# A selective scan's third output block, summed and copied out by other engines

## The chip, the cores and the metric

The kernel runs on one core of a Trainium2 chip. The metric is the device time of one execution in microseconds (us), the median of several runs. The core has five engines that run their own instruction queues in order[...]: TensorE (PE in the profile, its weight loads PEld), VectorE (DVE), ScalarE (ACT), GpSimd (POOL), and SyncE (SP), which here only issues DMA transfers.

## The reference

The input is eight images of 384 channels and 64 x 64 pixels, in fp32. Two layers follow each other, each of the form x + f(groupnorm(x)). The first f is an attention over channels with 1x1 and depthwise 3x3 convolutions. The second is a selective scan in four directions; the change lies there. In its code, cut down:

```python
xs = _cross_scan(x)                       # rows, columns, and both reversed
x_dbl = einsum('bkdl,kcd->bkcl', xs, x_proj_weight)
dts, Bs, Cs = split(x_dbl)                # 12, 16 and 16 channels
dt = softplus(einsum(dts, dt_projs_weight) + dt_projs_bias)
def step(h, inp):                         # over the 4096 places
    dA = exp(dt * A)
    h = h * dA + (dt * u)[..., None] * B
    y = einsum('bkdn,bkn->bkd', h, C)
ys = scan(step) + Ds * u
y = _cross_merge(ys)                      # the four directions are added
```

A layernorm over channels and a GELU end the layer. What matters here is the last line: the outputs of four sweeps over the image are summed place by place.

## The kernel before, in words

`selective_scan` handles one image. The loop is over 32 **steps**: four sweeps (k = 0 to 3; sweeps 2 and 3 run backwards), each over eight chunks of 512 places. Steps 0 to 7 are sweep 0, 8 to 15 sweep 1, and so on. In even sweeps the view of x is contiguous; in odd ones (columns) it is strided. A step has 12 **units**: three blocks of 128 channels (j) times four groups of four states (g). Unit r of a step is j = r // 4, g = r % 4.

For a unit, POOL forms the products db = w * B for its four states (`drive`, L910). ScalarE forms the decays da by an exponential, one per state (`decay`, L898), into one of three PSUM banks. VectorE runs the four scans (L922), each 512 places long, into h. One unit later TensorE transposes h in four banks of 4 x 128 columns (`turn`, L943; two banks in rotation), ScalarE copies each bank to SBUF as hc (`keep`, L949), and TensorE multiplies hc with the laid-out C and accumulates over the four groups into a PSUM bank py, one bank for each block j (`add_up`, L960). A direct term with D joins it in even sweeps (L966).

py has two banks, so a block's bank has to be emptied before the next block but one begins. `take` empties it: in sweep 0 VectorE copies it to SBUF (L1000); in later sweeps it adds it to the partial sum of the earlier sweeps (L1002). That sum has been fetched from memory into a buffer ysum by `sum_of` (L988, three buffers); the result is stored again (L986), and both go through SP's queue. The first two blocks of a step are taken in its unit 9, the third in the **next** step's unit 4.

Other work hangs on certain units. In units 0 to 3 TensorE projects the next step's x, three matmuls in each unit (`project`, L810), and reads x in the next step's view, so strided where the next step is in an odd sweep. In unit 4 ScalarE copies that projection out (`lay_out`, L818), and DMA spreads it as B and C. In unit 9, the burst, TensorE forms the next step's dt (L864, three 128x512 matmuls), ScalarE applies the softplus with two table loads (L872), and VectorE forms four tiles of C (L849). In steps 29 to 31 of all but the last image VectorE also collects the next image's statistics.

The order on each engine is written out by hand: `pin` keeps instructions in program order. Within a unit ScalarE alternates exponentials for two scans ahead with copies hc; VectorE's third scan of a unit needs the exponential issued just before that unit's first copy, and the fourth the one just after it:

```python
                turned(0)
                scanned(0)
                added(3, o - 1)
                if r == 4 and s > 0 and not last:
                    take(s - 1, 2)
                decay(i0 + 2)
                kept(0)
                turned(1)
```

Here `o` is the unit before. In units 0 to 3 the projection stands after `kept(1)`, ahead of the third transposes. DMA issues are not pinned.

Of the kernel before, what the change touches and what calls it, by code (L numbers as in the profile page):

```python
# [17 lines left out]
NJ = C // P  # L18
# [14 lines left out]
NG = N // NV  # L33
# [3 lines left out]
NLB = CH // P  # L37
# [58 lines left out]
def tile_channel_attention_then_selective_scan(ctx: ExitStack, tc: tile.TileContext, a: dict):  # L96
    nc = tc.nc
# [7 lines left out]
    ident = const.tile([P, P], F32, name="ident")  # L105
# [12 lines left out]
    for name in ("dt_bias", "Ds", "ln_w", "ln_b", "temp"):  # L118
        t = const.tile(list(a[name].shape), F32, name=name)
# [624 lines left out]
    def selective_scan(b, x1, stats1):  # L744

        y_d = dram.tile([L, C], F32, tag="yd", bufs=2, name=f"yd{b}")
        with ExitStack() as st:
# [6 lines left out]
            pin = tc.keep_in_program_order  # L754
# [11 lines left out]
            with tc.tile_pool(name=f"sn{b}", bufs=1, reuse_waits="tile") as np_:  # L766
# [4 lines left out]
                for c in range(5):  # L771
                    for j in range(NJ):
                        s = x1[j][:, bass.ts(c, CH)]
# [19 lines left out]
            steps = []  # L793
# [3 lines left out]
            S = len(steps)  # L797
# [85 lines left out]
            das, dbs, hs, hcs, pts, pys, carries, sums = {}, {}, {}, {}, {}, {}, {}, {}  # L883

            def place(u):

                s, r = divmod(u, UN)
                return s, *divmod(r, NG)
# [24 lines left out]
            def scan(u, v):  # L913
                s, j, g = place(u)
                k, c, start, end = steps[s]
                n = NV * g + v
                if v == 0:
                    hs[u] = work.tile([P, CH, NV], F32, tag="h", bufs=3, name=f"h{b}_{u}")
                da, db, h = das.pop(NV * u + v), dbs[u][:, v, :], hs[u][:, :, v]
                if k >= 2:  # L920
                    da, db, h = da[:, ::-1], db[:, ::-1], h[:, ::-1]
                pin(nc.vector.tensor_tensor_scan(  # L922
                    h, da, db, 0.0 if start else carries[s - 1][:, j, n : n + 1],
                    ALU.mult, ALU.add,
                ))
# [12 lines left out]
            def turn(u, lb):  # L938

                t = ps_t.tile([P, NF, P], F32, tag="t", name=f"pt{b}_{u}_{lb}")  # L940
                for f in range(NF):
                    q = NF * lb + f
                    pin(nc.tensor.transpose(t[:, f, :], hs[u][:, bass.ts(q, HP), :].rearrange("p l v -> p (l v)"), ident))  # L943
                pts[u, lb] = t

            def keep(u, lb):

                t = work.tile([P, NF, P], F32, tag="hc", bufs=6, name=f"hc{b}_{u}_{lb}")
                pin(nc.scalar.copy(t, pts.pop((u, lb))))  # L949
                hcs[u, lb] = t  # L950

            def add_up(u, lb):

                s, j, g = place(u)
                if g == lb == 0:
                    pys[s, j] = ps_y.tile([P, NLB, P], F32, tag="py", name=f"py{b}_{s}_{j}")
                hc, py = hcs.pop((u, lb)), pys[s, j]
                for f in range(NF):
                    q = NF * lb + f
                    pin(nc.tensor.matmul(  # L960
                        py[f * HP : (f + 1) * HP, lb, :], lhsT=cps[s, g][:, q, :], rhs=hc[:, f, :],
                        start=g == lb == 0, stop=g == NG - 1 and lb == NLB - 1,
                    ))
                k, c = steps[s][:2]
                if g == 1 and lb in SKIPS.get(k, ()):
                    pin(nc.tensor.matmul(  # L966
                        py[:, lb, :], lhsT=x1[j][:, c * CH + lb * P : c * CH + (lb + 1) * P],
                        rhs=skip[:, j, :], start=False, stop=False,
                    ))

            def rows(k, c, j):

                cs = bass.ts(j, P)
                if k % 2 == 0:
                    yield slice(0, P), y_d[bass.ts(c, CH), cs].rearrange("(l p) c -> p l c", p=P)
                    return
                v = y_d.rearrange("(h w) c -> h w c", w=W)[:, bass.ts(c, CH // H), cs]
                v = v.rearrange("h (l f) c -> f h l c", f=2)
                for f in range(2):
                    yield slice(f * H, (f + 1) * H), v[f]  # L980

            def move_y(s, j, t, store):
                k, c = steps[s][:2]
                for part, r in rows(k, c, j):
                    if store:
                        nc.sync.dma_start(r, t[part])  # L986
                    else:
                        nc.sync.dma_start(t[part], r)  # L988

            def sum_of(s, j):  # L990

                sums[s, j] = work.tile([P, NLB, P], F32, tag="ysum", bufs=3, name=f"ys{b}_{s}_{j}")
                if steps[s][0] > 0:
                    move_y(s, j, sums[s, j], False)

            def take(s, j):

                t = sums.pop((s, j))
                if steps[s][0] == 0:
                    pin(nc.vector.tensor_copy(t, pys.pop((s, j))))  # L1000
                else:
                    pin(nc.vector.tensor_add(t, t, pys.pop((s, j))))  # L1002
                move_y(s, j, t, True)
# [17 lines left out]
            for c in range(5, NCH):  # L1021
                for j in range(NJ):
                    s = x1[j][:, bass.ts(c, CH)]
# [36 lines left out]
            def unit(u):  # L1060

                o = u - 1
                s, r = divmod(u, UN)
                nxt = s + 1 < S
                last = u == U
                burst = r == 9 and nxt
                i0 = NV * u

                def scanned(v):
                    if not last:  # L1070
                        scan(u, v)

                def turned(lb):
                    if o >= 0:
                        turn(o, lb)

                def kept(lb):
                    if o >= 0:
                        keep(o, lb)

                def added(lb, of=o):
                    if of >= 0:
                        add_up(of, lb)

                if r in (2, 6, 10) and not last:
                    sum_of(s, r // 4)
                if not nxt and r in (8, 10) and not last:
                    take(s, (r - 8) // 2)
                if r >= 8 and nxt:
                    fetch(s + 1, r - 8)  # L1090

                if not last:
                    drive(u + 1)
                if u >= 2:
                    keep_last(u - 2)
                if r == 7 and nxt:
                    mingle_c(s + 1)
                if r == 10 and nxt:
                    weigh(s + 1, 0)
                if 0 < s < S and r in (0, 2):  # L1100
                    weigh(s, 1 + r // 2)

                turned(0)
                scanned(0)
                added(3, o - 1)
                if r == 4 and s > 0 and not last:
                    take(s - 1, 2)
                decay(i0 + 2)
                kept(0)
                turned(1)  # L1110
                if r == 8 and nxt:
                    turn_c(s + 1)
                scanned(1)
                decay(i0 + 3)
                if burst:
                    take(s, 0)
                    pd0 = step_matmul(s + 1, 0)
                    kept(1)
                    pd1 = step_matmul(s + 1, 1)
                    pd2 = step_matmul(s + 1, 2)  # L1120
                    added(0)
                    for j, pd in enumerate((pd0, pd1, pd2)):
                        step_size(s + 1, j, pd)
                    scanned(2)
                    scanned(3)
                    decay(i0 + 4)
                    for g in range(NG):
                        spread_c(s + 1, g)
                    take(s, 1)
                    added(1)  # L1130
                    turned(2)
                    decay(i0 + 5)
                    kept(2)
                    turned(3)
                    kept(3)
                    added(2)
                    return
                kept(1)
                if nxt and r < 4:
                    for i in range(3):  # L1140
                        project(s + 1, 3 * r + i)
                turned(2)
                added(0)
                scanned(2)
                decay(i0 + 4)
                kept(2)
                turned(3)
                added(1)
                if r == 4 and nxt:
                    lay_out(s + 1)  # L1150
                scanned(3)
                decay(i0 + 5)
                kept(3)
                added(2)
# [77 lines left out]
    for b in range(B):  # L1232
        x1, x1_d, stats1 = channel_attention(b, *x, before)
        y_d, x = selective_scan(b, x1, stats1)
        before = (b, x1_d, y_d)
# [50 lines left out]
```

## Time and profile before

| | us |
|---|---|
| median of 3 runs (19570.98 to 19581.24) | 19573.84 |
| the profiled execution's own time | 19593.03 |
| its span in the profile | 19591.2 |
| VectorE busy | 18453.4 (94%) |
| ScalarE busy | 17584.1 (90%) |
| TensorE busy | 17097.0 (87%) |
| GpSimd busy | 16874.4 (86%) |

A group in the profile is written as line, engine, operation, output <- inputs, shape and count; then the busy time in us, the mean of one in ns, and the idle time of the engine just before such instructions with what ended it. In the timeline the columns are start and duration in us, then the instructions merged (x4), with the idle time ahead of them in brackets. An fp32 matmul appears as two records[...]. TensorE's durations overlap each other; the distance between starts is what one costs.

### The profile page before, as it was taken

The page shows a single profiled execution, that of the slowest core. Times are in us where ns is not written, and L with a number is a line of the kernel's source. Part 1 is how long each engine was busy: PE and PEld are TensorE (multiplying, and loading weights), DVE is VectorE, ACT ScalarE, POOL GpSimd, SP SyncE. Part 2 cuts the span into 40 slices and gives each one's busy share as a digit, 9 for nine tenths or more (in the row PEclk, how much of TensorE's full clock was granted, in tenths as well). Part 3 has the DMA queues.
Part 4 walks back from the last instruction along what each step waited for, and adds up shares of the span by engine and source line. Part 5 has one row for each costly group of instructions (what it writes and reads, how often), then busy time and mean ns, then how long its engine had stood idle before and what let it go on. Part 6 is the DMA issues. An engine that isn't in the chain of part 4 may idle for free.

```text
span 19591.2 us, 415258 instructions
## 1 busy us (share of the span) xinstructions
PE 17097.0 (87%) x166560; PEld 10219.2 (52%) x166560; DVE 18453.4 (94%) x17510; ACT 17584.1 (90%) x30011; POOL 16874.4 (86%) x7486
## 2 busy tenths in 40 slices
PE   7888888888888888888888888888888888888887
PEld 4555545555455554555545555455554555545554
DVE  7999989999899998999989999899998999989998
ACT  6999979999799987999879998899988999889998
POOL 4999959999599985999859998599985999869997
PEclk9999999999999999999999999999999999999998
DMA  1232322223222232232322323223232223322223
GB/s 47 84 97 97 112 89 83 94 97 111 91 86 94 95 109 89 87 97 96 109 85 87 97 97 108 85 87 97 97 108 92 83 95 97 106 93 88 94 93 124
DMA packets 1214410, 1849.25 MB, mean 94 GB/s; under 512 B 154209, under 2 KB 1018721, under 8 KB 1075265
## 3 DMA queue, kind: packets, MB, share of 16 engines
q1 hardware_dynamic: 1211616, 1822.57, 28.7%
q8 instruction: 1314, 21.53, 0.5%
q14 instruction: 616, 5.04, 0.1%
q10 hardware_dynamic: 864, 0.12, 0.0%
HBM read 1503.58 MB, written 318.77 MB: 93 GB/s over the span
## 4 chain that ended last, share of the span: by engine, by line
ACT 27%; PE 23%; DVE 15%; issue 4%; POOL 3%; DMA 1%; SPq 0%; DVEq 0%; ACTq 0%; POOLq 0%
ACT da L898 12%; ACT hc L949 10%; PE pt L943 10%; DVE h L922 10%; PE py L960 5%; PE px L810 3%; DVE ac L451 3%; POOL db L910 2%; ACT dt L872 1%; PE pp L599 1%; PE pd L864 1%; PE py L966 1%; ACT pr L413 1%; ACT L872 1%; ACT L898 1%
## 5 line engine op out<-in xcount | busy, mean ns | idle before, releaser
L910 POOL TENSOR_TENSOR db<-w,B 128x2048 f32<-128x2048 f32 x3072 | 14053.0, 4578 | 618.8 <-DVE h L922 514.7
L922 DVE TENSOR_TENSOR_SCAN h<-da,ca,db 128x512 f32<-128x512 f32 x10752 | 12786.6, 1263 | 305.3 <-ACT da L898 287.0
L898 ACT ACTIVATE da<-dt,neg_a 128x512 f32<-128x512 f32 x12288 | 8741.8, 713 | 157.6 <-DVE h L922 153.4
L943 PE MATMUL pt<-ident,h 128*128 128x128 f32 x49152 | 8127.0, 294 | 858.4 <-DVE h L922 505.8
L949 ACT COPY hc<-pt 128x512 f32<-128x512 f32 x12288 | 7393.0, 604 | 704.7 <-PE pt L943 641.1
L943 PEld LDWEIGHTS pt<-ident,h 128*128 128x128 f32 x49152 | 5452.3, 146 | 3314.2 <-issue 1912.0
L960 PE MATMUL py<-hc,cp 128*32 128x128 f32 x98304 | 5070.4, 290 | 893.4 <-ACT hc L949 726.0
L960 PEld LDWEIGHTS py<-hc,cp 128*32 128x32 f32 x98304 | 2050.1, 110 | 3164.5 <-ACT hc L949 1607.1
L922 DVE TENSOR_TENSOR_SCAN h<-da,db 128x512 f32<-128x512 f32 x1536 | 1748.2, 1206 | 115.8 <-ACT da L898 73.5
L420 POOL TENSOR_TENSOR pr<-pr,pr 128x1008 f32<-128x1008 f32 x288 | 673.3, 2338 | 1201.1 <-ACT pr L413 1184.0
L810 PE MATMUL px<-x,wx 128*44 128x128 f32 x6144 | 1219.8, 343 | 36.9 <-DVE cp L849 21.3
L881 POOL TENSOR_TENSOR w<-x,dt 128x512 f32<-128x512 f32 x744 | 1062.4, 1428 | 33.4 <-ACT dt L872 31.9
L810 PEld LDWEIGHTS px<-x,wx 128*44 128x44 f32 x6144 | 687.4, 128 | 367.0 <-issue 190.0
L864 PE MATMUL pd<-xd,wdt 128*128 128x512 f32 x1536 | 731.8, 613 | 157.0 <-DVE h L922 151.2
L426 POOL TENSOR_TENSOR pr<-pr,pr 128x1008 f32<-128x1008 f32 x288 | 574.8, 1996 | 277.2 <-ACT pr L413 193.8
L849 DVE TENSOR_TENSOR cp<-quad,pct 128x512 f32<-128x512 f32 x1024 | 628.2, 674 | 10.9 <-PE pct L838 10.9
L599 PE MATMUL pp<-v,mT 128*128 128x512 f32 x1152 | 539.1, 618 | 92.5 <-DVE v L456 91.4
L872 ACT ACT_TABLE_LOAD x256 | 328.4, 1283 | 229.1 <-PE pd L864 228.1
L936 POOL COPY ca<-h 128x4 f32<-128x4 f32 x2688 | 531.6, 198 | 0.0
L864 PEld LDWEIGHTS pd<-xd,wdt 128*128 128x128 f32 x1536 | 272.3, 190 | 465.4 <-issue 239.2
L872 ACT ACTIVATE dt<-pd,dt_bias 128x512 f32<-128x512 f32 x768 | 475.0, 686 | 8.2 <-PE pd L864 4.4
L1002 DVE TENSOR_TENSOR ys<-ys,py 128x512 f32<-128x512 f32 x576 | 383.9, 667 | 34.6 <-PE py L960 34.6
(334 smaller groups left out, 11500.5 us busy)
## 6 DMA issues: line engine op xcount, KB each, us to landing
B<-bcd SPq DMA_DIRECT2D x1024, 1024.0 KB, 4.8
yd<-ys SPq DMA_DIRECT2D x384, 256.0 KB, 3.4
ys<-yd SPq DMA_DIRECT2D x768, 128.0 KB, 2.9
yd<-ys SPq DMA_DIRECT2D x768, 128.0 KB, 4.3
x<-in_x SPq DMA_DIRECT2D x48, 1024.0 KB, 7.2
x1d<-x SPq DMA_DIRECT2D x192, 256.0 KB, 2.8
ys<-yd SPq DMA_DIRECT2D x192, 256.0 KB, 3.0
fy<-yd SPq DMA_DIRECT2D x128, 384.0 KB, 3.8
```

The lines of the kernel that those rows point to most:

```text
L420: pin(nc.gpsimd.tensor_add(q[:, :, 1:], q[:, :, 1:], left[:, :, : W - 1]))
L599: pin(nc.tensor.matmul(pps[m, c], lhsT=fold_of[0][:, j, bass.ts(m, P)], rhs=vs["v"][:, j, bass.ts(c, CH)], start=j == 0, stop=j == NJ - 1,))
L810: pin(nc.tensor.matmul(split(pxs[s][:XR, :])[:, part, :], lhsT=wx[:, j, k, :], rhs=view(x1[j], k, c)[:, part, :], start=i == 0, stop=i == ...
L864: pin(nc.tensor.matmul(pd, lhsT=wdt[:, k, bass.ts(j, P)], rhs=xds[s], start=True, stop=True))
L872: pin(nc.scalar.activation(dts[s, j], pd, AF.Softplus, bias=small["dt_bias"][:, j, k : k + 1]))
L881: pin(eng.tensor_mul(split(ws[s, j]), view(x1[j], k, c), split(dts[s, j])))
L898: pin(nc.scalar.activation(t, dts[s, j], AF.Exp, scale=neg_a[:, j, steps[s][0], n : n + 1]))
L910: pin(eng.tensor_mul(t, w.broadcast_to([P, NV, CH]), bts[s, g]))
L922: pin(nc.vector.tensor_tensor_scan(h, da, db, 0.0 if start else carries[s - 1][:, j, n : n + 1], ALU.mult, ALU.add,))
L943: pin(nc.tensor.transpose(t[:, f, :], hs[u][:, bass.ts(q, HP), :].rearrange("p l v -> p (l v)"), ident))
L949: pin(nc.scalar.copy(t, pts.pop((u, lb))))
L960: pin(nc.tensor.matmul(py[f * HP : (f + 1) * HP, lb, :], lhsT=cps[s, g][:, q, :], rhs=hc[:, f, :], start=g == lb == 0, stop=g == NG - 1 an ...
```

## The change

The third block of every step that is followed by another, so 31 of 32 in each image, is no longer taken by VectorE in unit 4. In sweeps 1 to 3 TensorE adds the fetched partial sum to the bank py in unit 1 of the next step, as a matmul with the identity, 128x512 fp32, that closes the accumulation. In unit 2 ScalarE copies the bank into the same ysum buffer, and the store follows. In sweep 0 there is nothing to add, and only the copy moves to ScalarE. The first two blocks of a step, and the last step's third, are taken as before.

```diff
                 hc, py = hcs.pop((u, lb)), pys[s, j]
+                full = g == NG - 1 and lb == NLB - 1 and not summed_by_pe(s, j)
...
-                        start=g == lb == 0, stop=g == NG - 1 and lb == NLB - 1,
+                        start=g == lb == 0, stop=full,
...
+            def summed_by_pe(s, j):
+                return j == NJ - 1 and s < S - 1 and steps[s][0] > 0
+
+            def sum_by_pe(s, j):
+
+                if summed_by_pe(s, j):
+                    pin(nc.tensor.matmul(
+                        pys[s, j].rearrange("p b c -> p (b c)"), lhsT=ident,
+                        rhs=sums[s, j].rearrange("p b c -> p (b c)"), start=False, stop=True,
+                    ))
+
+            def take_by_act(s, j):
+
+                t = sums.pop((s, j))
+                pin(nc.scalar.copy(t, pys.pop((s, j))))
+                move_y(s, j, t, True)
...
                 added(3, o - 1)
-                if r == 4 and s > 0 and not last:
-                    take(s - 1, 2)
+                if r == 1 and s > 0:
+                    sum_by_pe(s - 1, 2)
                 decay(i0 + 2)
                 kept(0)
+                if r == 2 and s > 0 and not last:
+                    take_by_act(s - 1, 2)
                 turned(1)
```

## The prediction

> **What bounds the kernel now.** I read the page's engine shares and groups first.
>
> ```profile
> PE 17097.0 (87%) x166560; PEld 10219.2 (52%) x166560; DVE 18453.4 (94%) x17510; ACT 17584.1 (90%) x30011; POOL 16874.4 (86%) x7486
> ...
> L922 DVE TENSOR_TENSOR_SCAN h<-da,ca,db 128x512 f32<-128x512 f32 x10752 | 12786.6, 1263 | 305.3 <-ACT da L898 287.0
> ...
> L949 ACT COPY hc<-pt 128x512 f32<-128x512 f32 x12288 | 7393.0, 604 | 704.7 <-PE pt L943 641.1
> ...
> L1002 DVE TENSOR_TENSOR ys<-ys,py 128x512 f32<-128x512 f32 x576 | 383.9, 667 | 34.6 <-PE py L960 34.6
> ```
>
> VectorE is fullest, and inside the scan it almost never rests: 12288 scans leave 421 us of gaps (305.3 + 115.8, the first steps' scans). Next the list of waits, to see what makes those gaps:
>
> ```profile
> ACT hc L949 <- PE pt L943: 641.1, 1283, 3.6
> ...
> DVE h L922 <- ACT da L898: 360.5, 791, 2.6
> ```
>
> VectorE waits for ScalarE's exponential, and ScalarE, in order, waits for TensorE's transposes. The timeline says where. TensorE in unit 2 of step 12 of the fourth image (next step in sweep 1, whose x view is strided):
>
> ```profile
> 8517.92 0.66 PE L943 MATMUL pt<-ident,h 128*128 128x128 f32 x4
> 8518.50 0.43 PE L960 MATMUL py<-hc,cp 128*32 128x128 f32 x8
> 8518.86 0.66 PE L943 MATMUL pt<-ident,h 128*128 128x128 f32 x4
> 8519.45 0.65 PE L960 MATMUL py<-hc,cp 128*32 128x128 f32 x16
> 8520.02 0.66 PE L943 MATMUL pt<-ident,h 128*128 128x128 f32 x4
> 8520.61 0.43 PE L960 MATMUL py<-hc,cp 128*32 128x128 f32 x8
> 8520.97 0.65 PE L943 MATMUL pt<-ident,h 128*128 128x128 f32 x4
> 8521.55 1.48 PE L810 MATMUL px<-x,wx 128*44 128x128 f32 x6
> 8522.96 0.66 PE L943 MATMUL pt<-ident,h 128*128 128x128 f32 x4
> ```
>
> No gap: the same transpose returns after 8522.96 - 8517.92 = 5.04 us, of which 1.41 are the projection (L810), while VectorE's four scans take 4 x 1.175 = 4.70. So in units 0 to 3 of such a step TensorE is the slowest; ScalarE waits for it once a unit:
>
> ```profile
> 8523.71 0.59 ACT L949 COPY hc<-pt 128x512 f32<-128x512 f32 x1 [0.55 <-PE pt L943]
> ```
>
> VectorE then reaches unit 4 with hardly any exponential in hand:
>
> ```profile
> 8529.69 0.66 DVE L1002 TENSOR_TENSOR ys<-ys,py 128x512 f32<-128x512 f32 x1
> 8530.27 5.98 DVE L922 TENSOR_TENSOR_SCAN h<-da,ca,db 128x512 f32<-128x512 f32 x5
> ```
>
> The fifth of these scans starts at 8534.99; its exponential ran 8534.09 to 8534.80: 0.19 in hand. Where the next step's view is contiguous, three projections take 0.78, a unit costs TensorE about 4.4, and VectorE runs unbroken to the add and past it (step 18):
>
> ```profile
> 8871.95 24.79 DVE L922 TENSOR_TENSOR_SCAN h<-da,ca,db 128x512 f32<-128x512 f32 x21 [0.40 <-ACT da L898]
> 8896.66 0.66 DVE L1002 TENSOR_TENSOR ys<-ys,py 128x512 f32<-128x512 f32 x1
> ```
>
> There exponentials lie ready about 1.0 us early in unit 2 and 1.1 in unit 5. From unit 6 on all steps are VectorE's; unit 9's burst sets ScalarE back to VectorE's pace. So a step's change is what VectorE has lost or won by unit 5.
>
> [...]
>
> **The change, part by part.** Per image, steps 1 to 31 have the third block's take moved: 31 x 8 = 248.
>
> Removed: one VectorE operation in unit 4. Its 0.66 overlaps the next scan; on the path it is 8530.27 - 8529.69 = 0.58 us. 248 x 0.58 = 144 us, if VectorE can use it.
>
> Added to TensorE, in steps 9 to 31 (184 times): a 128x512 fp32 matmul in unit 1, after the last py of the old block and ahead of the second transposes. The nearest row is L864 (same shape): [...]their weight loads 0.43 apart, so 0.86 us. Ends: 0.75 (some overlap) to 1.1 (a wait for the loaded y in front of it). I take 0.86. Behind it stand transposes, ScalarE's copies, then exponentials, then scans. The y that it reads was fetched some nine units earlier, in unit 4 of the step before, so its landing is no limit.
>
> Added to ScalarE: a copy PSUM to SBUF 128x512 in unit 2, between a copy hc and an exponential, 248 times. L949's next instruction starts 0.48 after it[...], and L949's mean is 604. I take 0.48 (0.45 to 0.6).
>
> Moved: the store of the block (one DMA issue, two in odd sweeps) on SP, from behind VectorE's add in unit 4 to behind ScalarE's copy in unit 2. Behind it in SP's queue stand the load into the same ysum buffer and the bcd store, whose data come from ScalarE in unit 4 as before; both can only go earlier. The py bank and the ysum buffer come free two units sooner. POOL's instructions and their order stay, and its products are finished 1.1 us or more, mostly 3 us, before their scan; a step shorter by 0.58 takes no more than that from the lead each time, and POOL idles about 2 us per step (514.7 us for VectorE over 256 steps) to make it up. I cost all these at nothing; with that cover gone, each us that POOL is late would be one of the step.
>
> Now VectorE's delay by unit 5, step by step (- is a gain). "In hand" is a scan's start less the end of its exponential, as the timeline before has them, in means over the eight images.
> - Steps 1 to 6: no matmul. ScalarE is 0.48 late, and 0.7 or more lies ready: hidden. -0.58 each, 6 steps, -3.5.
> - Steps 7 and 8: no matmul, strided. The 0.55 gap swallows the copy, but exponentials are only 0.03 early in unit 5 already, so the freed 0.58 is waited away. 0.
> - Steps 9 to 14 and 25 to 28: TensorE full, strided. In unit 2 ScalarE is 0.86 + 0.48 late; the 0.55 gap takes the copy's share back, 0.86 stays. VectorE is 0.86 late in unit 3, wins 0.58 back in unit 4, and loses it in unit 5: 0.14 in hand on average, of which 0.03 is the least ever seen, so 0.86 - 0.11 = +0.75. 10 steps, +7.5.
> - Steps 15 and 17 to 22: contiguous. ScalarE has no gap in unit 2: transposes come 0.86 later, 0.3 of it spare, plus 0.48: 1.1 late against 1.0 in hand, so VectorE loses about 0.2 and wins 0.58. -0.38, 7 steps, -2.7.
> - Step 16 (first of its sweep, short scans, 0.5 in hand throughout, so ScalarE never gets ahead): some 1.0 late less 0.5, +0.5.
> - Steps 23 and 24: strided, nothing in hand: +0.86 each, +1.7.
> - Steps 29 to 31: the next image's statistics on VectorE, or no projection, give TensorE room: -0.4 each, -1.2.
>
> Sum: -3.5 + 7.5 - 2.7 + 0.5 + 1.7 - 1.2 = +2.3 us per image, 8 images +18; the last image has no statistics, so two steps of +0.75 instead of -0.4, +2. Together **+20 us** on the profiled 19591.2 (its run took 19593.03, 0.1% above the median of the three, whose instructions are the same). On the median: 19573.84 + 20 = **19594 us**, +0.1%. A change of 0.2% (39 us) is about what can be told from none.
>
> **Rivals.**
> That the change does what it says is not in doubt: the order of the changed program's instructions has the 184 matmuls and 248 copies where the text says.
>
> 1. *VectorE's relief is kept* (faster): TensorE takes the matmul in slack that the estimated ends hide. For it: VectorE 94%, TensorE 87%. Against it: starts without a gap, ScalarE's 0.55. Then the ten strided steps give -0.11 each, the seven contiguous ones -0.58, steps 29 to 31 -0.53, and 16, 23 and 24 nothing: (-3.5 - 1.1 - 4.1 - 1.6) x 8 = -82, 19492 us. With every 0.58 kept, 19430.
> 2. *ScalarE's copy goes on the path too* (slower): in the 12 strided steps with a matmul the copy isn't swallowed by the gap, as ScalarE is late already. For it: copy and matmul meet in unit 2. Against: the gap follows the copy. It decides once ScalarE's lateness exceeds TensorE's by the gap. 12 x 8 x 0.48 = 46 more: 19640 us.
> 3. *The matmul costs more than its like*, 1.1: 20 steps x 8 x 0.24 = 38 more: 19632 us.
>
> **How the numbers follow.** The exchange as worked out 0.47; rival 1 and half-way to it 0.22; rivals 2 and 3 0.31. These are the chances of within 0.2%, faster and slower. Range: towards rival 1 to -60 (19514), and a little past rival 2, +75 (19649).
>
> **What would show it.** Groups: VectorE's adds 392 instead of 576 and its copies 128 instead of 192, TensorE 184 new matmuls, ScalarE 248 new copies of about 0.6. Starts on TensorE around a new matmul 0.86 apart; VectorE's waits for the exponential up from 360 us to some 500; strided steps (9 to 14) longer by 0.7, steps 1 to 6 shorter by 0.6. I am wrong if strided steps don't lengthen (rival 1), if they lengthen by 1.2 (rival 2), or if POOL's products become what scans wait for.

## The result and the profile after

The changed kernel takes 19618.19 us (median of 13 runs, 19597.24 to 19631.56) against 19576.08 (13 runs, 19562.87 to 19585.97) for the kernel before: a ratio of 1.0022, 95% interval 1.0014 to 1.0029. It is 0.2% slower, 42 us. Its profiled execution spans 19629.7 us, 38.5 more than before.

The page of the changed kernel, engine shares and groups:

```profile
PE 17318.7 (88%) x166928; PEld 10283.8 (52%) x166928; DVE 18347.5 (93%) x17262; ACT 17660.3 (90%) x30259; POOL 16878.0 (86%) x7486
...
L922 DVE TENSOR_TENSOR_SCAN h<-da,ca,db 128x512 f32<-128x512 f32 x10752 | 12801.8, 1263 | 419.4 <-ACT da L898 382.6
...
L949 ACT COPY hc<-pt 128x512 f32<-128x512 f32 x12288 | 7427.1, 607 | 709.2 <-PE pt L943 663.4
```

VectorE is busy 106 us less (18453.4 before), and its idle time before scans grew by 139 us (305.3 + 115.8 before; 419.4 here, and 140.8 in the group of the first steps). What it was spared it spends waiting, and more. TensorE's busy time grew by 222 us, ScalarE's by 76. The list of waits names the same pair as before, the first larger by 114 us:

```profile
DVE h L922 <- ACT da L898: 474.4, 1047, 2.6
```

The two new groups, in the list of groups (184 matmuls, two records each, and 248 copies; the transposes of L943 leave one record each):

```profile
L1003 PE MATMUL py<-ys,ident 128*128 128x512 f32 x368 | 207.1, 645 | 0.0
...
L1011 ACT COPY ys<-py 128x512 f32<-128x512 f32 x248 | 151.0, 609 | 0.0
```

Now the same step as in the prediction, step 12 of the fourth image, whose projection is strided ("strided steps" are those that project for a step of an odd sweep, "contiguous" the others). TensorE's timeline in unit 1:

```profile
8520.19 0.42 PE L961 MATMUL py<-hc,cp 128*32 128x128 f32 x8
8520.54 1.12 PE L1003 MATMUL py<-ys,ident 128*128 128x512 f32 x2
8521.50 0.60 PE L943 MATMUL pt<-ident,h 128*128 128x128 f32 x4
```

The second transposes start 0.96 us after the new matmul. Not all of that is the matmul's, for these transposes are followed after 0.53 us (8522.03 - 8521.50), where before it was 0.58 (8521.55 - 8520.97): from unit 1's first to its third transposes, the median over the steps is 2.94 us before and 3.84 after in strided steps, 2.31 and 3.22 in contiguous ones. So the matmul costs TensorE 0.906 us in both. ScalarE a little later, in units 1 and 2:

```profile
8522.20 0.59 ACT L949 COPY hc<-pt 128x512 f32<-128x512 f32 x1 [0.56 <-PE pt L943]
...
8524.19 0.58 ACT L949 COPY hc<-pt 128x512 f32<-128x512 f32 x1 [0.82 <-PE pt L943]
...
8526.87 0.60 ACT L1011 COPY ys<-py 128x512 f32<-128x512 f32 x1
...
8529.23 0.59 ACT L949 COPY hc<-pt 128x512 f32<-128x512 f32 x1
```

Before, it waited once a unit, 0.55 us ahead of the third copy hc. In unit 1 it now waits twice, 0.56 for the transposes right behind the matmul and 0.82 for the third ones, so it falls some 0.83 further behind. In unit 2 it copies the block out (8526.87), and the third copy hc (8529.23) hardly waits any more: over the strided steps this gap is 0.06 us on average, 0.55 before. The copy fills a gap that was there. And VectorE, in units 1 to 4:

```profile
8523.46 1.29 DVE L922 TENSOR_TENSOR_SCAN h<-da,ca,db 128x512 f32<-128x512 f32 x1 [0.37 <-issue]
8525.41 2.46 DVE L922 TENSOR_TENSOR_SCAN h<-da,ca,db 128x512 f32<-128x512 f32 x2 [0.66 <-ACT da L898]
8528.10 7.17 DVE L922 TENSOR_TENSOR_SCAN h<-da,ca,db 128x512 f32<-128x512 f32 x6 [0.23 <-ACT da L898]
8535.49 1.28 DVE L922 TENSOR_TENSOR_SCAN h<-da,ca,db 128x512 f32<-128x512 f32 x1 [0.22 <-ACT da L898]
```

The add is gone, and four scans wait, 1.48 us in all. The contiguous step 18 of that image looks quite different:

```profile
8879.09 33.01 DVE L922 TENSOR_TENSOR_SCAN h<-da,ca,db 128x512 f32<-128x512 f32 x28 [0.59 <-ACT da L898]
```

28 scans in a row, through the place where the add was.

For the rest of this section and the next, one measure: the distance from a step's first scan to the first scan of its unit 10, in the trace of a run less that of the kernel before, as a mean over steps and images. Units 10 and 11 are left out, for a reason told at the end. In us per step:

| steps | 1-6 | 7, 8 | 9-14, 25-28 | 15, 17-22 | 16 | 23, 24 | 29-31 |
|---|---|---|---|---|---|---|---|
| predicted | -0.58 | 0 | +0.75 | -0.38 | +0.5 | +0.86 | -0.4 |
| changed kernel | -0.53 | -0.13 | +0.86 | -0.34 | +0.65 | +0.98 | -0.37 |

Over all steps and images this comes to +34 us of the 38.5. In the runs below the means of a column scatter from image to image by some 0.1 us, at most 0.2; that of step 16 by up to 0.3, those of steps 29 to 31 by 0.2 to 0.6.

### The profile page after: what moved, and what is told of

Same layout as the page of the kernel before. It is cut to its first block, busy times and chain, and to the rows that moved or that the text cites. A ratio compares the mean times of both kernels' runs of the same rounds, so it can differ in the third digit from the quotient of the medians.

```text
span 19629.7 us, 416220 instructions
## 1 busy us (share of the span) xinstructions
PE 17318.7 (88%) x166928; PEld 10283.8 (52%) x166928; DVE 18347.5 (93%) x17262; ACT 17660.3 (90%) x30259; POOL 16878.0 (86%) x7486
## 4 chain that ended last, share of the span: by engine, by line
ACT 39%; PE 33%; DVE 15%; issue 7%; POOL 3%; DMA 1%; SPq 0%; DVEq 0%; ACTq 0%; POOLq 0%
ACT da L898 17%; ACT hc L949 16%; PE pt L943 13%; DVE h L922 8%; PE py L961 7%; PE px L810 5%; DVE ac L451 4%; POOL db L910 3%; PE pp L599 2%; ACT dt L872 2%; PE pd L864 1%; ACT pr L413 1%; PE py L1003 1%; ACT L872 1%; PE py L967 1%
## 5 line engine op out<-in xcount | busy, mean ns | idle before, releaser
L910 POOL TENSOR_TENSOR db<-w,B 128x2048 f32<-128x2048 f32 x3072 | 14057.8, 4579 | 629.9 <-DVE h L922 522.3
L922 DVE TENSOR_TENSOR_SCAN h<-da,ca,db 128x512 f32<-128x512 f32 x10752 | 12801.8, 1263 | 419.4 <-ACT da L898 382.6
L943 PE MATMUL pt<-ident,h 128*128 128x128 f32 x49152 | 8144.6, 294 | 658.8 <-DVE h L922 283.7
L949 ACT COPY hc<-pt 128x512 f32<-128x512 f32 x12288 | 7427.1, 607 | 709.2 <-PE pt L943 663.4
L943 PEld LDWEIGHTS pt<-ident,h 128*128 128x128 f32 x49152 | 5459.7, 145 | 3195.4 <-issue 1757.2
L922 DVE TENSOR_TENSOR_SCAN h<-da,db 128x512 f32<-128x512 f32 x1536 | 1752.9, 1208 | 140.8 <-ACT da L898 91.8
L599 PEld LDWEIGHTS pp<-v,mT 128*128 128x128 f32 x1152 | 219.6, 198 | 358.1 <-issue 238.9
```

The source lines that it names most:

```text
L599: pin(nc.tensor.matmul(pps[m, c], lhsT=fold_of[0][:, j, bass.ts(m, P)], rhs=vs["v"][:, j, bass.ts(c, CH)], start=j == 0, stop=j == NJ - 1,))
L910: pin(eng.tensor_mul(t, w.broadcast_to([P, NV, CH]), bts[s, g]))
L922: pin(nc.vector.tensor_tensor_scan(h, da, db, 0.0 if start else carries[s - 1][:, j, n : n + 1], ALU.mult, ALU.add,))
```

## The experiments

Theory: in strided steps TensorE sets the pace, so the matmul costs its full length there and VectorE's relief is worth nothing; elsewhere the relief counts. Rivals: ScalarE's copy is what costs; the relief counts everywhere and something larger eats it; the losses travel from step to step. All eight kernels were timed against the kernel before on their own chip (19574.11 and 19578.22 us), in four to sixteen runs each.

| kernel | us | ratio to before | 1-6 | 7, 8 | 9-14, 25-28 | 15, 17-22 | 16 | 23, 24 | 29-31 |
|---|---|---|---|---|---|---|---|---|---|
| no_matmul | 19497.56 | 0.9963 (0.9951-0.9976) | -0.55 | -0.16 | -0.02 | -0.56 | -0.07 | -0.09 | -0.38 |
| matmul_vector_copy | 19719.89 | 1.0075 (1.0063-1.0088) | -0.01 | -0.03 | +1.00 | +0.05 | +0.64 | +0.87 | +0.26 |
| moved_where_free | 19533.81 | 0.9979 (0.9971-0.9987) | -0.55 | -0.06 | +0.01 | -0.32 | -0.07 | -0.02 | -0.20 |
| moved_where_full | 19678.12 | 1.0052 (1.0039-1.0066) | +0.05 | -0.01 | +0.90 | +0.05 | -0.08 | +0.81 | +0.10 |
| projection_spread | 19533.52 | 0.9978 (0.9971-0.9986) | -0.59 | -0.65 | +0.27 | -0.53 | +0.17 | +0.19 | -0.36 |
| sum_in_unit_4 | 19676.11 | 1.0051 (1.0038-1.0063) | -0.62 | +0.46 | +1.08 | -0.34 | +0.74 | +1.25 | +0.19 |
| before_spread | 19509.5 | 0.9966 (0.9954-0.9979) | -0.02 | -0.70 | -0.46 | +0.06 | 0.00 | -0.71 | +0.14 |
| free_and_spread | 19425.13 | 0.9922 (0.9909-0.9936) | -0.62 | -0.63 | -0.46 | -0.50 | -0.08 | -0.66 | -0.24 |

The same distance, ended earlier, takes the parts of the change apart: up to the first scan of unit 4 VectorE has not yet been spared anything, up to that of unit 6 it has. Strided steps are here 9 to 14 and 25 to 28, contiguous ones 15 and 17 to 22:

| | strided, to unit 4 | to unit 6 | contiguous, to unit 4 | to unit 6 |
|---|---|---|---|---|
| changed kernel | +0.97 | +0.87 | +0.27 | -0.33 |
| no_matmul | +0.09 | -0.01 | 0.00 | -0.60 |
| matmul_vector_copy | +1.00 | +1.00 | 0.00 | 0.00 |
| projection_spread | +0.52 | +0.28 | +0.07 | -0.53 |
| before_spread | -0.46 | -0.46 | 0.00 | 0.00 |
| sum_in_unit_4 | +0.05 | +1.09 | 0.00 | -0.33 |

**no_matmul.** The matmul alone is taken out of the changed kernel, so the earlier sweeps' sum is missing from the third blocks.

```diff
             def summed_by_pe(s, j):
-                return j == NJ - 1 and s < S - 1 and steps[s][0] > 0
+                return False
```

> The change with TensorE's matmul left out: ScalarE still copies the third block out in unit 2, and VectorE's operation in unit 4 is gone, but the earlier sweeps' partial sum is not added to that block. Theory (the matmul is what costs, because TensorE sets the pace in units 0 to 3 of strided steps): those steps are no longer lengthened and gain about 0.1 us each, contiguous ones 0.58, so about 82 us below the kernel before (-0.4%), some 124 us below the changed kernel. Rival (ScalarE's copy is what costs there): strided steps keep 0.5 us or more, so 12 x 8 x 0.5 = 48 us less gain, about 35 us below the kernel before.

Measured: 77 us below before, 82 expected by the theory. In the strided steps -0.02: not lengthened, but nothing is won either, although VectorE does 0.58 us less in each. The step's sum alone would allow that the copy costs about as much as the relief gives. The distance to unit 4 rules that out: before any relief the steps are only 0.09 late, so ScalarE's copy isn't what costs. The list of waits of this kernel shows ScalarE waiting for TensorE less than in either of the two kernels (641.1 before, 663.4 after):

```profile
ACT hc L949 <- PE pt L943: 521.7, 1029, 3.6
```

So the matmul makes the difference between -77 and +42 us.

**matmul_vector_copy.** The matmul alone is kept; VectorE copies in unit 4 for as long as it added before.

```diff
+                if r == 4 and s > 0 and not last:
+                    take_summed(s - 1, 2)      # nc.vector.tensor_copy, then the store
-                if r == 2 and s > 0 and not last:
-                    take_by_act(s - 1, 2)
```

> TensorE's matmul stays in unit 1, but VectorE copies the bank in unit 4 (as long as its add was) and ScalarE copies nothing. Theory: VectorE's relief is worth nothing in strided steps, so the 12 strided steps with a matmul stay about 0.9 us longer than before, as in the changed kernel; contiguous ones are level with before; step 16 up to 0.4 longer. 11 to 11.5 us an image, about 90 us above before (+0.45%). Rival (the relief counts in every step, and the changed kernel is slow by the sum of both): 144 us above the changed kernel, about 186 above before (+0.95%).

Measured: 146 us above before, between the two expectations, so the total decides nothing. The steps do. Up to unit 4 the strided ones are +1.00 without the copy and +0.97 with it, so the copy adds nothing there. Up to unit 6 they are +1.00 and +0.87: of VectorE's 0.58 only 0.10 is kept. In contiguous steps the matmul alone costs nothing, and so does the copy alone (no_matmul); both together cost 0.27, and the relief gives 0.60, all of it. In steps 1 to 6 the whole step is -0.01 against -0.53. That strided steps lengthen by 1.00 here, 0.09 more than the matmul's 0.906, is not explained.

Units 0 to 9 hold 108 us of the loss and units 10 and 11 another 15, together all but 2 of the 125 us between the two traces. The medians are 21 us further apart than the traces, because the profiled execution of before was 19 us slower than that kernel's median and that of this kernel 2 us faster than its own.

**moved_where_free** and **moved_where_full** split the change by steps: a list of the blocks that are moved, the others taken as before.

```diff
+MOVED = (0, 1, 2, 3, 4, 5, 14, 16, 17, 18, 19, 20, 21, 28, 29, 30)   # moved_where_free
+MOVED = (8, 9, 10, 11, 12, 13, 22, 23, 24, 25, 26, 27)               # moved_where_full
             def summed_by_pe(s, j):
-                return j == NJ - 1 and s < S - 1 and steps[s][0] > 0
+                return j == NJ - 1 and s in MOVED and steps[s][0] > 0
...
+                if r == 4 and s > 0 and not last and s - 1 not in MOVED:
+                    take(s - 1, 2)
...
-                if r == 2 and s > 0 and not last:
+                if r == 2 and s > 0 and not last and s - 1 in MOVED:
```

> The change only where TensorE has room: third blocks of steps 0 to 5, 14, 16 to 21 and 28 to 30; in all others VectorE adds in unit 4 as before. Theory: steps 1 to 6 gain 0.58 each, 15 and 17 to 22 about 0.45, 29 to 31 about 0.35, the rest as before: -7.7 us an image, 60 us below the kernel before (-0.3%). Rival (what is lost in strided steps isn't local, but given on from step to step, so the gains are too): no more than the gain of the whole exchange, level with before or above it.

> The complement of moved_where_free: the change only for the third blocks of steps 8 to 13 and 22 to 27, whose takes fall into the 12 strided steps where TensorE is full. Theory: each of those steps lengthens by 0.86 in units 1 to 5, all others stay: 12 x 8 x 0.86 = 83 us above before (+0.4%), and with moved_where_free it adds up to the whole change. Rival (the steps act on each other): the two don't add up.

Measured: -40 and +100 us, against -60 and +83. The signs and the places are those of the theory: steps that were left alone stay within 0.1 us, strided ones with the change lengthen by 0.90 and 0.81, the free ones shorten nearly as in the whole change (steps 29 to 31 less, -0.20 against -0.37, but they scatter most). So a step's loss or gain stays in the step. Both sums came out some 20 us too high; together they make +60, where the whole change makes +42, and the intervals (about 16 us to each side for the first, 26 for the second) allow that. In the traces, units 0 to 9 of all steps make -51 and +92 us, together +41, against +34 for the whole change. The rival that losses travel from step to step falls.

**projection_spread.** The whole change, with the cause I named thinned out: fewer projections in units 1 to 3.

```diff
-                if nxt and r < 4:
-                    for i in range(3):
-                        project(s + 1, 3 * r + i)
+                if nxt and r < 5:
+                    for i in range((0, 3, 5, 7, 9)[r], (3, 5, 7, 9, 12)[r]):
+                        project(s + 1, i)
```

> The whole change, with the next step's twelve projections spread as 3, 2, 2, 2, 3 over units 0 to 4 instead of 3 in each of units 0 to 3. This takes 1.41 us of strided projection from TensorE in units 1 to 3 and puts it into unit 4. Theory (TensorE's pace in units 0 to 3 is the cause): strided steps fall from +0.95 to about +0.4 against before, some 50 us below the changed kernel, level with before or a little under. Rival (ScalarE's copy or the place of the matmul is the cause): the strided steps stay +0.9, the time that of the changed kernel.

Measured: 41 us below before, and 83 below the changed kernel, each against its own runs of before; I had expected 50 below the latter. Matmul and copy stand where they stood, and the strided steps fall from +0.86 to +0.27. By itself this doesn't show that TensorE's load made the matmul dear: the spread can be worth that much without the matmul, which the next run asks.

**before_spread** asks what the spread is worth by itself. Its edit is the one above, in the kernel before.

> The kernel before, third block and all, with the projections alone spread as 3, 2, 2, 2, 3 over units 0 to 4. Theory: VectorE's waits for the exponential in units 2 to 5 of the 14 strided steps go, 0.3 us a step and 0.6 or more in steps 7, 8, 23 and 24: about 43 us below before (-0.2%). Rival (the spread helps only by making room for the matmul): level with before.

Measured: 69 us below before, where I expected 43; nothing in contiguous steps, -0.46 in strided ones, -0.7 in 7, 8, 23 and 24. So the kernel before already lost that much to TensorE in its strided steps, and VectorE's wait shrinks accordingly:

```profile
DVE h L922 <- ACT da L898: 304.4, 604, 2.6
```

It was 360.5 before, with 791 waits.

So most of what projection_spread won in strided steps is the spread's own. Measured against before_spread, the change still lengthens them by 0.27 + 0.46 = 0.73, hardly less than 0.86, and steps 23 and 24 by 0.90. A rough estimate suggests why: a strided projection takes 1.41 / 3 = 0.47 us, so with two of them instead of three a unit costs TensorE 5.04 - 0.47 = 4.57 us, still close to the 4.70 of VectorE's scans. It is in the contiguous steps that the spread made room for the matmul: up to unit 4 they are +0.07 instead of +0.27, although the spread alone does nothing there. There the load on TensorE is shown to matter for what the matmul costs; in strided steps this spread was too small to show it. As a whole the change on top of the spread wins nothing: projection_spread is 28 us above before_spread, with intervals that overlap.

**sum_in_unit_4** keeps the load and moves the new work out of the projections' way.

```diff
-                if r == 1 and s > 0:
+                if r == 4 and s > 0 and not last:
                     sum_by_pe(s - 1, 2)
...
-                if r == 2 and s > 0 and not last:
-                    take_by_act(s - 1, 2)
...
                 kept(2)
+                if r == 4 and s > 0 and not last:
+                    take_by_act(s - 1, 2)
```

> The whole change, but three units later: the matmul in unit 4 instead of 1 and ScalarE's copy after unit 4's third copy hc, so both behind the projections. Theory (the matmul costs because it stands in TensorE's full stretch): in strided steps only ScalarE's 0.48 remains, less the 0.11 in hand, +0.4 instead of +0.86; contiguous steps give the whole 0.58. About 30 us below before, 70 below the changed kernel. Rival (matmul and copy cost wherever they stand): as the changed kernel, 40 above before.

A miss: 98 us above before, and worse than the change itself. ScalarE's timeline in unit 4 of step 12, fourth image:

```profile
8557.11 0.59 ACT L949 COPY hc<-pt 128x512 f32<-128x512 f32 x1 [0.56 <-PE pt L943]
8557.59 0.70 ACT L898 ACTIVATE da<-dt,neg_a 128x512 f32<-128x512 f32 x1
8558.21 0.59 ACT L949 COPY hc<-pt 128x512 f32<-128x512 f32 x1
8558.69 0.59 ACT L1011 COPY ys<-py 128x512 f32<-128x512 f32 x1
8559.16 0.58 ACT L818 COPY xd<-px 44x512 f32<-44x512 f32 x1
```

The first line is a wait that wasn't there before: the matmul stands right ahead of the second transposes, and ScalarE's copy of them waits 0.56. The projections don't make this wait, for over the contiguous steps it is as long, 0.58 on average, as over the strided ones, 0.56. Then the copy (0.47 to the next start) and the projection's copy (0.48) follow each other, and no gap comes after that could swallow them. 0.56 + 0.47 is 1.03; the strided steps lengthened by 1.08. The contiguous ones lose only 0.27 of their 0.60, as in the changed kernel, for their exponentials lie ready about 1.1 us early. So my theory, that the matmul costs because it stands in the full units 0 to 3, was too narrow: what counts is whether exponentials lie ready, and in strided steps they hardly do in units 4 and 5 either: in the kernel before, the first scan of unit 4 finds its exponential 0.27 us early there and the second of unit 5 0.14, against 1.31 and 1.14 in contiguous steps.

In unit 2 the copy costs next to nothing (strided steps of no_matmul are 0.09 late at unit 4), because the next transposes are late there anyway, by 0.55 before; in unit 4 it costs its whole length, 0.47. Steps 7 and 8, which have the copy but no matmul, show it alone: +0.46 here, -0.13 in the changed kernel. Rival 2 of the prediction is right in unit 4, and wrong in unit 2. The matmul's share in unit 4, 1.08 - 0.46 = 0.62, is a difference between groups of steps; no run has the matmul alone there.

**free_and_spread** is both: the spread, and the change in steps 1 to 8, 15, 17 to 22 and 29 to 31 only.

> Both: projections spread, and the change only in steps 1 to 8, 15, 17 to 22 and 29 to 31. If the two effects are separate they add: steps 1 to 6 and 15 to 22 -0.5 to -0.6, strided ones -0.3 to -0.6, 13.7 us an image, about 110 us below before (-0.55%).

Measured: 153 us below before (110 expected), ratio 0.9922, interval 0.9909 to 0.9936. The steps are nearly those of its parts: -0.46 in strided steps as in before_spread, -0.50 in contiguous ones, so the two effects are separate. It beats both kernels. The two traces are 166 us apart; 35 of these lie in units 10 and 11 and are not explained by it. VectorE in step 12 of the fourth image, an add left in place:

```profile
8432.06 21.27 DVE L923 TENSOR_TENSOR_SCAN h<-da,ca,db 128x512 f32<-128x512 f32 x18
8453.24 0.66 DVE L1021 TENSOR_TENSOR ys<-ys,py 128x512 f32<-128x512 f32 x1
8453.82 8.33 DVE L923 TENSOR_TENSOR_SCAN h<-da,ca,db 128x512 f32<-128x512 f32 x7
```

No wait from unit 0 to unit 5.

## Why the prediction was right

The forecast was +20 us, "within 0.2%" with 0.47 and "slower" with 0.31; measured are +42 us, 0.22%, in the range and at the very edge between the two. The +20 itself lies below the measured interval (27 to 57 us). The mechanism held, step by step; the sum was too small.

- *Removed, 0.58 where VectorE can use it*: right. Steps 1 to 6 got -0.60 up to unit 6, and so did contiguous steps in no_matmul; strided ones got -0.01 there.
- *The matmul, 0.86*: 0.906 measured on TensorE. In front of 120 of the 184, those whose y comes from an odd sweep, the records show a separate wait, 51 ns long; but the others cost 0.906 too, so the wait isn't what I missed.
- *Strided steps, +0.75*: +0.86. This is the term of the sum that was mis-sized most, 10 steps x 8 x 0.11 = 9 us. The path was right: late up to unit 4, a part of the relief kept, the rest waited away in unit 5. I had 0.86 late less 0.11 kept; the trace has 0.97 less 0.10 (+0.97 to unit 4, +0.87 to unit 6). So the lateness was too small. The matmul's 0.05 is part of it; the other 0.06 stays open. The copy isn't it, for matmul_vector_copy has +1.00 without it.
- *Contiguous steps, -0.38*: -0.34. I had matmul and copy take 0.2 from VectorE together; they took 0.27, and neither took anything alone.
- *Steps 16, 23, 24, +0.5 and +0.86*: +0.65 and +0.98. *Steps 29 to 31, -0.4*: -0.37.
- *Moved stores and POOL at nothing*: right; the products' wait for VectorE is 522.3 us (514.7 before), and scans wait for POOL no more than before (36.3 us in the first steps' group, 35.8 before).
- *VectorE's wait up from 360 to some 500*: 474.4.
- *Rival 1*, the relief kept because TensorE has hidden slack: no, strided steps lengthened; its -82 us is about what came when the matmul was left out (-77). *Rival 2*: wrong where the copy stands, as ScalarE's gap of 0.06 instead of 0.55 and the distances to unit 4 show. *Rival 3*, 1.1 for the matmul: no, 0.906.

The measured 42 us is 22 more than forecast. The differences between the first two rows of the step table, each times its number of steps, make 1.9 us an image, so 15 us, of which 9 are the strided steps'. All but that of steps 7 and 8 point the same way. The other 7 are well inside the interval, 15 us to each side.

## What to carry to other kernels

The share of busy time named VectorE, and relieving it was worth next to nothing (0.10 of 0.58 us) in the steps where TensorE's queue had no gap between starts (5.04 us a unit against VectorE's 4.70): look at the stretch in which the work would land, not at the whole, before moving it to a less busy engine. The same copy cost next to nothing ahead of a wait that existed anyway (unit 2, -0.13 us in steps 7 and 8), and its whole length where none followed (unit 4, +0.46). Thinning out the full stretch (two projections a unit instead of three) gave more, 69 us, than moving the work even where that paid, 40 us, and the two then added up step by step (-0.46 us in strided steps, -0.50 in contiguous ones). It did not make the strided steps fit for the move: there the exchange still cost 0.73 us a step.

## What the runs showed of the hardware that was not expected

The first unit after the burst, unit 10, varies from step to step with TensorE's granted clock. Windows of unit 10 of steps 9 and 10 in the fourth image of the kernel before (length, busy time of each engine, granted clock, DMA share and rate):

```profile
8375.85:8381.56 5.71, 4.64 (x40) 3.10 (x40) 4.92 (x4) 4.54 (x9) 3.87 (x3) 0.70 0.71 210
8438.54:8443.27 4.73, 3.60 (x48) 2.32 (x48) 4.73 (x5) 4.70 (x9) 3.57 (x2) 1.00 0.70 201
```

With the clock at 1.00 the unit takes 4.73 us, VectorE's own pace; at 0.70 it takes 5.71, as the scans wait (0.39 us ahead of the fourth, 0.40 ahead of the next unit's first). Over the trace 208 of 248 such units ran below 0.95 and took 5.34 us on average, the other 40 ran at 1.00 and took 4.69. In the burst TensorE stands idle for no more than 2.48 us at a time, 2.47 in step 9 as in step 10, and 2.47 on average ahead of the 208 units as of the 40, so the length of this idle stretch doesn't tell them apart; what decides which units are hit, no run here tested. Between the kernels' traces units 10 and 11 together differ from before by -35 to +17 us, which is why they were kept out of the step table, and why I don't read a difference of some 20 us in a total as an effect of the edit.
